# A selective scan on five engines: which products GpSimd takes, where ScalarE changes its tables, and a C of three groups

## The chip, the cores and the metric

The kernel runs on one core of a Trainium2 chip. A core has five engines with instruction queues of their own: PE (TensorE, matrix products into PSUM), DVE (VectorE), ACT (ScalarE, functions from tables), POOL (GpSimd) and SP (which issues the transfers, DMAs, here). Each works through its queue in order; semaphores tie the queues together. The metric is the device time of one execution in microseconds (us); lower is better.

## The reference, cut to what matters

The program is a chain of four layers on an image of 2 x 128 x 64 x 64. The change touches layer 0 alone, a Mamba block run over the image in four directions (the convolution and the splits written short here):

```python
def _mamba(x, W_in, conv_w, conv_b, W_xp, W_dt, b_dt, A_log, Dp, W_out):
    xz = x @ W_in.T
    xh, z = jnp.split(xz, 2, axis=-1)
    xc = causal_conv4(xh) + conv_b
    xh = silu(xc)
    dt, Bm, Cm = split(xh @ W_xp.T)          # 8, 16, 16 columns
    dt = softplus(dt @ W_dt.T + b_dt)
    A = -jnp.exp(A_log)
    dA = jnp.exp(dt[..., None] * A)
    dBu = dt[..., None] * Bm[:, :, None, :] * xh[..., None]
    h = dA_t * h + dBu_t                     # scan over L, 16 states a channel
    y = jnp.einsum('lbdn,bln->bld', hs, Cm)
    y = y + xh * Dp
    y = y * silu(z)
    return y @ W_out.T
...
x_norm = _layernorm(x_flat, ln_w, ln_b)
# four directions: rows forward, rows backward, columns forward, columns backward
fused = jnp.concatenate([out_tl_br, out_br_tl, out_tr_bl, out_bl_tr], axis=-1)
x = fused @ W_fuse.T + b_fuse
```

The length L is 4096, d_inner is 256, the batch is 2. Layers 1 and 2 are attention blocks, layer 3 a smaller Mamba.

## The kernel before

**Chunks.** Layer 0 is cut into 64 chunks of 512 positions: 2 images x 2 orders (rows, columns) x 2 senses (`rev`) x 8 chunks, one after the other in that order. The state `hst` is carried from a chunk to the next of its direction.

**Units and steps.** 256 channels x 16 states are 4096 scans; a *unit* is 1024 columns on 128 partitions (two scans of 512 side by side), so a chunk has 16 units u = 0 to 15. Unit u belongs to the group of states g = u % 8 // 2 (four states) and to the quarter of the channels q = u // 8 * 2 + u % 2. A chunk has 16 *steps*; step s contains scan s and the work that stands around it for other units. What one unit goes through:

- `s_dbu` (L381, product at L384, POOL): dbu = dus x B, for unit s + 2, into one of NDBU = 3 buffers, so that dbu(u) must wait until scan(u - 3) is done.
- `s_da` (L386, L397, ACT): da = exp(dt A), two instructions of 512, for unit s + 1, into one of two PSUM tiles, so that da(u) must wait for scan(u - 2).
- `s_fix` (L400, L412, ACT): adds the carried state at the seam into dbu(u); it needs dbu(u). For group 0 it makes `df` first (L409).
- `s_scan` (L420, L428, DVE): the scan itself, into one of NH = 3 buffers h.
- `s_hst` (L430, L433, ACT): keeps the last state, of unit s - 1.
- `s_hc` (L435): hc = h x C, of unit s - 1. For the units in `POOL_HC` POOL makes it (L438), with C as rows spread by transfers into `cs`; for the others DVE does (L440), with C in a PSUM tile `pc` that PE makes from a selection matrix (`s_pc`, L417).
- `s_y` (L447, L451, PE): adds hc into the PSUM accumulator y, two units at a time, in the step that the table `pairs` names: two steps behind a unit of DVE, three behind one of POOL. The two halves of y share one bank; `y0` (L442, L444, steps 3 and 11) begins a half with D x xs, and `yg_` (L455, L458, DVE) takes it out with the gate.

**The rest of a chunk, spread over the steps.** While chunk `c` scans, parts of the next chunk (`new`) and of the one behind it (`nxt`) are made in the same 16 steps, and the last half of `old`'s result leaves. Four tables say which: `A[s]` on ACT (behind da, fix and hst of step s), `M[s]` on PE, `V[s]` on DVE (right behind scan s) and `G[s]` on POOL. They hold: the projection of dt for `new` (`pt`, L341, PE; `abs_`, `e_exp`, `e_ln`, ACT; `dt_`, DVE; `dtu_`, POOL), the gate (`pz`, `z_`, `zsilu` in forward chunks, `zload` in backward ones), the convolution of `nxt` (`px`, L282, four products of two instructions each on PE; `x_`, L291, ACT; `xsilu`, L305, ACT; `pd`, L321, PE), the output of `old` (`po`, L469 and L473, PE; `xo`, L478 or L480, ACT), and in some chunks the layer norm (`lp`, `ln`), and `turn` (L255, 16 chunks), which lays the normed image out by columns. All PE results of this kind go through a single PSUM bank, `misc`: a product into it waits until the one before has been read. The tile `xs` of each half has two buffers for the three chunks in work, so that `nxt`'s `x_(i)` overwrites what `y0(i)` of `c` reads.

**Table visits.** ACT's exponentials all come from one table. Ln (`e_ln`, L354) and Silu (`zsilu`, L309; `xsilu`, L305) come from others; each is a visit: a load of the other table, the function, and a load back.

**Transfers.** SP spreads the rows of B and C (`states`, L331, L335: four transfers of 64 KB a group) and dt and dt x u (`spread`, L371, L376) over the partitions for `new`. C's groups are loaded in the order of `GROUPS_C`, in steps 11, 12, 13 and 15, into as many `cs` buffers.

Within a step the order of issue is: s_dbu, s_scan, V, s_hc, G, y0, s_y, s_da, s_fix, s_hst, A, M, s_pc, yg_, transfers.

Of the kernel before, what the change touches and what calls it, by code (L numbers as in the profile page):

```python
# [13 lines left out]
P = 128  # L14
B, C, H, W = 2, 128, 64, 64
L = H * W
T = 512
NCH = L // T
NS = 16
POOL_HC = (0, 5, 9, 11, 14)  # L20
GROUPS_C = (0, 2, 1, 3)
NHC, NH, NDBU = 4, 3, 3
ND3 = 6
ND = 73
# [28 lines left out]
def _bc(ap, axis, shape):  # L53
    return ap.unsqueeze(axis).to_broadcast(shape)
# [3 lines left out]
def conv_seq_kernel(ctx: ExitStack, tc: tile.TileContext, a: dict, out: bass.AP):  # L58
# [40 lines left out]
    with ExitStack() as c0:  # L99
# [9 lines left out]
        def wt(tag, bufs=None, shape=(P, 2, T)):  # L109
            return wk_.tile(list(shape), F32, tag=tag, name=tag, bufs=bufs)  # L110
# [87 lines left out]
        def gq(u):  # L198

            return u % 8 // 2, u // 8 * 2 + u % 2  # L200
# [52 lines left out]
        def turn(j):  # L253

            nc.scalar.copy(  # L255
                xnt[:, 3 + j * T : 3 + (j + 1) * T].rearrange("p (w h) -> p w h", h=H),
                xn[:, 3 : L + 3].rearrange("p (h w) -> p w h", w=W)[:, 8 * j : 8 * j + 8, :],
            )

        class Chunk:  # L260
# [69 lines left out]

            def states(self, j, g):  # L331

                t = wt("cs" if j else "bs", len(GROUPS_C) if j else 4, (P, T))
                for n in range(4):
                    nc.sync.dma_start(t[32 * n : 32 * n + 32, :],  # L335
                                      self.rows[j, 4 * g + n, :].partition_broadcast(32))
                (self.cs if j else self.bs)[g] = t
# [97 lines left out]
            def s_hc(self, u):  # L435
                t = self.hc[u] = wt("hc", NHC)
                if u in POOL_HC:
                    nc.gpsimd.tensor_mul(t, self.h[u], _bc(self.cs[gq(u)[0]], 1, [P, 2, T]))  # L438
# [51 lines left out]
        turns = {k: k % 8 for k in (*range(8, 16), *range(32, 40))}  # L490
# [3 lines left out]
        for u in range(0, 16, 2):  # L494
            pairs.setdefault(max(m + (3 if m in POOL_HC else 2) for m in (u, u + 1)), []).append(u)

        with tc.manual_schedule():
            c, c1 = chunks[:2]
# [78 lines left out]
            c.dtu_(1)  # L577
            for g in GROUPS_C:
                c.states(1, g)
# [31 lines left out]
            old = None  # L611
            for k, c in enumerate(chunks):
                new, nxt = (chunks[k + i] if k + i < nk else None for i in (1, 2))
                ln, lp = norms.get(k), norms.get(k - 1)

                def at(u):
                    return (c, u) if 0 <= u < 16 else ((old, u + 16) if u < 0 else (new, u - 16))

                A, V, M, G = {}, {}, {}, {}
                if old is not None:
                    M[2], A[4] = old.po, (old.xo,)
                if c.rev:
                    A[4] = (*A[4], c.zload)
                else:
                    A[8] = (c.zsilu,)
                if new is not None:
                    if lp is not None:
                        A[0] = (new.xd_,)  # L630
                    M[0], A[1] = lambda: new.pt(0), (lambda: new.abs_(0),)
                    M[1], A[2] = lambda: new.pt(1), (lambda: new.abs_(1), new.e_exp)
                    A[3] = (new.e_ln,)
                    M[4], V[5] = lambda: new.pt(0), lambda: new.dt_(0)
                    M[5], V[6] = lambda: new.pt(1), lambda: new.dt_(1)
                    G[7], G[8] = lambda: new.dtu_(0), lambda: new.dtu_(1)
                    if not new.rev:
                        M[6], A[7] = lambda: new.pz(0), (lambda: new.z_(0),)
                        M[13], A[14] = lambda: new.pz(1), (lambda: new.z_(1),)
                if nxt is not None:  # L640
                    M[9], A[10] = lambda: nxt.px(0), (lambda: nxt.x_(0),)
                    M[10], A[12] = lambda: nxt.px(1), (lambda: nxt.x_(1),)
                    A[13] = (nxt.xsilu,)
                    M[15] = nxt.pd
                if lp is not None:
                    A[3] = (*A[3], lp.ln, lp.exp)
                    A[6] = (lp.rows,)
                    M[7], V[8] = lp.scale, lp.mul
                    A[10] = (lp.affine, *A.get(10, ()))
                if ln is not None:  # L650
                    M[12], V[13] = ln.center, ln.sub
                    A[14] = (*A.get(14, ()), ln.square)
                    M[14], A[15] = ln.var, (ln.keep,)
                if 7 <= k < 11:
                    w1, w2 = (Low((k - 7) // 2, (k - 7) % 2, hf) for hf in range(2))
                    M[6], A[7] = w1.conv, (w1.out,)
                    M[13], A[14] = w2.conv, (w2.out, *A.get(14, ()))
                if 11 <= k < 15:
                    sl = slice(2 * T * (k - 11), 2 * T * (k - 10))
                    nc.sync.dma_start(x[:, 1, sl], xin[:, 1, sl])  # L660
                if k in turns:
                    A[11] = (lambda: turn(turns[k]),)

                for s in range(16):
                    (c1, u1), (c2, u2), (cp, up) = at(s + 1), at(s + 2), at(s - 1)

                    if c2 is not None:
                        c2.s_dbu(u2)
                    c.s_scan(s)
                    if s in V:  # L670
                        V[s]()
                    if cp is not None:
                        cp.s_hc(up)
                    if s in G:
                        G[s]()

                    if s in (3, 11):
                        c.y0(s // 11)
                    for cy, e in ((c, s), (old, s + 16)):
                        for u in pairs.get(e, ()) if cy is not None else ():  # L680
                            cy.s_y(u)
                            cy.s_y(u + 1)

                    if s == 0 and new is not None and lp is None:
                        new.xd_()
                    if c1 is not None:
                        c1.s_da(u1)
                        c1.s_fix(u1)
                    if cp is not None:
                        cp.s_hst(up)  # L690
                    for f in A.get(s, ()):
                        f()

                    if s in M:
                        M[s]()
                    if s % 2 and s < 15:
                        c.s_pc(s + 1)
                    elif s == 15 and new is not None:
                        new.s_pc(0)

                    if s == 1 and old is not None:
                        old.yg_(1)
                    if s == 10:
                        c.yg_(0)

                    if new is not None:
                        if s in (7, 14):
                            new.spread("dts", s // 14)
                        if s in (9, 13):
                            new.spread("dus", s // 13)  # L710
                        if s in (8, 10, 12, 14):
                            new.states(0, s // 2 - 4)
                        if s in (11, 12, 13, 15):
                            new.states(1, GROUPS_C[{11: 0, 12: 1, 13: 2, 15: 3}[s]])
                old = c
            c.s_hc(15)
            for e in (16, 17):
                for u in pairs.get(e, ()):
                    c.s_y(u)
                    c.s_y(u + 1)  # L720
# [12 lines left out]
    with ExitStack() as c1:  # L733
# [308 lines left out]
        for n, j in enumerate(jobs):  # L1042
# [10 lines left out]
            if jobs[n - 1].layer == 1:  # L1053
                for ci in range(NCH):
                    c = Conv(jobs[n - 1].b, ci)
# [4 lines left out]
        with tc.manual_schedule():  # L1060
# [22 lines left out]
            for slot in range((len(groups) + 2) * UPG):  # L1083
                u = slot % UPG
                G = at(slot)[0]
                if G is not None:
                    G.score(u)
                    nxt = at(slot + UPG)[0]
# [39 lines left out]
    with ExitStack() as c3:  # L1128
# [302 lines left out]
        cs = [(c, k, u) for c, k in steps for u in range(2 if k == 0 else 4)]  # L1431
# [26 lines left out]
        with tc.manual_schedule():  # L1458
            mm(y, lhsT=ident, rhs=x[:, 0, 0:T], start=True, stop=True)
            c, c1 = chunks[:2]  # L1460
# [22 lines left out]
            for s in range(-1, len(steps) + 3):  # L1483
                (pc_, pk), (cc, ck), (nc_, nk) = at(s - 1), at(s), at(s + 1)
                (n2, n2k) = at(s + 2)
                ci, k = divmod(s, 4)
                fut = chunks[ci + 1] if s >= 0 and ci + 1 < len(chunks) else None
                fut2 = chunks[ci + 2] if ci + 2 < len(chunks) else None
                old = chunks[ci - 1] if ci > 0 else None
# [216 lines left out]
```

## Time and profile before

| | us |
|---|---|
| median of 3 runs | 6571.11 (6571.02 to 6574.9) |
| the profiled execution, its own time | 6584.95 |
| its span, first to last instruction | 6583.0 |
| first scan of layer 0 to last scan of layer 0, start | 57.7 to 3468.3 |

Busy time in the stretch that holds layer 0's scans, 57 to 3470 us (3413 us):

| engine | busy us | instructions |
|---|---|---|
| PE | 2900.20 | 7790 |
| DVE | 3271.05 | 2004 |
| ACT | 2744.18 | 5241 |
| POOL | 3324.06 | 1470 |

The groups of instructions of layer 0 that matter here, on the whole span:

| line, engine, what | count | mean ns | idle before, us |
|---|---|---|---|
| L384 POOL dbu | 1024 | 2450 | 101.0 |
| L438 POOL hc | 320 | 2394 | 1.1 |
| L428 DVE scan, with a carried state | 896 | 2347 | 93.0 |
| L440 DVE hc | 704 | 1203 | 10.6 |
| L397 ACT da | 2048 | 689 | 347.6 |
| L412 ACT fix | 896 | 377 | 77.8 |
| L451 PE y | 4096 | 758 | 194.9 |

A row of the view by lines gives the source line, the engine, the number of instructions, the mean time of one, and how long the engine had been idle right before them. The view of waits names the engine that ended such idle time ("DVE h L428 <- ACT dbu L412" is a scan that waited for ACT's fix), with the total, the number and the longest. The timeline lists start, duration, engine, line and tiles, neighbours of one kind merged ("x2"), and in brackets the idle time before. Consecutive instructions of an engine overlap a little, so that the step from one start to the next is a little shorter than the duration shown.

### The profile page before, as it was taken

How to read it: one execution, taken by the hardware profiler on the slowest of the kernel's cores; microseconds unless marked ns; L12 is line 12 of the kernel's file. 1: busy time of each engine (PE TensorE's matmuls, PEld its weight loads, DVE VectorE, ACT ScalarE, POOL GpSimd, SP SyncE). 2: the span in 40 equal slices, each digit the busy share in tenths (PEclk: the TensorE clock that was granted, in tenths of full speed). 3: DMA queues.
4: the chain of work that ended last, by engine and by line, in shares of the span. 5: the costliest groups of instructions: out<-in, count | busy, mean ns of one | idle time of the engine just before them, and what ended most of it. 6: DMA issues, size and time to landing. Idle time of an engine off the chain costs nothing. (4 is left out here: it accounts for less than half of the span.)

```text
span 6583.0 us, 66639 instructions
## 1 busy us (share of the span) xinstructions
PE 5814.1 (88%) x20014; PEld 2782.5 (42%) x20014; DVE 5608.2 (85%) x4530; ACT 4490.9 (68%) x7772; POOL 5458.0 (83%) x2553
## 2 busy tenths in 40 slices
PE   8888888888888888888888999999999998788897
PEld 2222222222222222222216888888888887122221
DVE  7999999999999999999996666666666676699998
ACT  7887778877788777887776565555555555445543
POOL 6999999999999999999995666655666666688887
PEclk7888788877788777887779999999999999689888
DMA  6566655566665666556550000000000000777775
GB/s 182 146 154 161 161 142 145 147 150 150 152 152 150 151 152 151 146 145 150 149 140 19 2 4 3 1 1 1 1 1 1 1 1 1 191 176 179 186 181 135
DMA packets 400476, 700.62 MB, mean 106 GB/s; under 512 B 74089, under 2 KB 76530, under 8 KB 399730
## 3 DMA queue, kind: packets, MB, share of 16 engines
q1 hardware_dynamic: 399232, 694.33, 42.8%
q8 instruction: 157, 2.57, 0.2%
q14 instruction: 205, 1.68, 0.1%
q10 hardware_dynamic: 882, 2.04, 0.1%
HBM read 584.80 MB, written 111.28 MB: 106 GB/s over the span
## 5 line engine op out<-in xcount | busy, mean ns | idle before, releaser
L384 POOL TENSOR_TENSOR dbu<-dus,bs 128x1024 f32<-128x1024 f32 x1024 | 2464.5, 2450 | 101.0 <-DVE h L428 86.2
L428 DVE TENSOR_TENSOR_SCAN h<-da,hst,dbu 128x1024 f32<-128x1024 f32 x896 | 2096.3, 2347 | 93.0 <-ACT dbu L412 88.1
L397 ACT ACTIVATE da<-dts,aneg 128x512 f32<-128x512 f32 (+1 forms) x2048 | 1410.2, 689 | 347.6 <-DVE h L428 309.8
L924 POOL TENSOR_TENSOR sum<-sum,sc 128x1024 f32<-128x1024 f32 x384 | 910.3, 2371 | 504.1 <-ACT sc L919 500.3
L886 ACT COPY sc<-s 128x512 f32<-128x512 f32 x1024 | 596.7, 584 | 780.0 <-PE s L881 645.5
L881 PE MATMUL s<-q,k 128*128 128x256 f32 x4096 | 1052.8, 380 | 6.3 <-ACT q L838 3.0
L451 PE MATMUL y<-hc,cst 128*32 128x512 f32 x4096 | 884.9, 758 | 194.9 <-DVE hc L440 175.6
L936 PE MATMUL av<-sc,v 128*128 128x256 f32 x4096 | 1049.0, 379 | 3.6 <-ACT sc L919 3.6
L893 DVE TENSOR_TENSOR mx<-mx,s 128x512 f32<-128x512 f32 x896 | 610.2, 681 | 453.0 <-ACT sc L886 450.1
L440 DVE TENSOR_TENSOR hc<-h,pc 128x1024 f32<-128x1024 f32 x704 | 847.0, 1203 | 10.6 <-PE y L451 8.7
L881 PEld LDWEIGHTS s<-q,k 128*128 128x128 f32 x4096 | 777.3, 191 | 120.1 <-issue 6.2
L936 PEld LDWEIGHTS av<-sc,v 128*128 128x128 f32 x4096 | 768.5, 190 | 104.6 <-ACT sc L919 5.4
L438 POOL TENSOR_TENSOR hc<-h,cs 128x1024 f32<-128x1024 f32 x320 | 766.0, 2394 | 1.1 <-issue 1.1
L417 PE MATMUL pc<-xd,sel 16*128 16x512 f32 x1024 | 709.9, 784 | 1.5 <-DVE hc L440 1.3
L1323 POOL TENSOR_TENSOR A<-A,D 128x1024 f32<-128x1024 f32 x224 | 526.5, 2369 | 132.3 <-DVE D L1328 105.0
L916 DVE TENSOR_TENSOR sc<-sc,pm 128x1024 f32<-128x1024 f32 x512 | 621.1, 1214 | 0.9 <-PE pm L912 0.9
L919 ACT ACTIVATE sc<-sc 128x1024 f32<-128x1024 f32 x512 | 542.0, 1059 | 23.8 <-DVE sc L916 23.3
L341 PE MATMUL misc<-xd,w_dt 9*128 9x512 f32 x504 | 374.5, 831 | 140.3 <-ACT x L480 78.1
L451 PEld LDWEIGHTS y<-hc,cst 128*32 128x32 f32 x4096 | 125.8, 120 | 852.0 <-DVE hc L440 414.8
L412 ACT ACTIVATE dbu<-hst,dbu,df 128x1 f32<-128x1 f32 x896 | 337.9, 377 | 77.8 <-POOL dbu L384 55.5
L1340 PE MATMUL q<-xs,lc 32*128 32x512 f32 x896 | 302.0, 682 | 75.4 <-DVE A L1346 74.0
L417 PEld LDWEIGHTS pc<-xd,sel 16*128 16x128 f32 x1024 | 183.1, 219 | 351.9 <-issue 301.8
(280 smaller groups left out, 7753.8 us busy)
## 6 DMA issues: line engine op xcount, KB each, us to landing
dts<-ddt SPq DMA_DIRECT2D x512, 256.0 KB, 5.4
dus<-ddu SPq DMA_DIRECT2D x512, 256.0 KB, 5.0
D<-rows SPq DMA_DIRECT2D x448, 256.0 KB, 5.7
bs<-rows SPq DMA_DIRECT2D x1024, 64.0 KB, 4.9
cs<-rows SPq DMA_DIRECT2D x1024, 64.0 KB, 3.2
ddt<-dt SPq DMA_DIRECT2D x128, 256.0 KB, 2.0
ddu<-dtu SPq DMA_DIRECT2D x128, 256.0 KB, 4.0
dtr<-ddt SPq DMA_DIRECT2D x448, 64.0 KB, 2.1
```

The lines of the kernel that those rows point to most:

```text
L384: nc.gpsimd.tensor_mul(t, self.dus[q], _bc(self.bs[g], 1, [P, 2, T]))
L397: act(t[:, i, sl], self.dts[q][:, i, sl], AF.Exp, scale=an[:, g, 2 * q + i : 2 * q + i + 1])
L417: mm(t, lhsT=sel[32:48, 4 * g : 4 * g + 4, :].rearrange("p n d -> p (n d)"), rhs=self.xd[32:48, :], start=True, stop=True)
L428: nc.vector.tensor_tensor_scan(ho, ai, bi, init, ALU.mult, ALU.add)
L438: nc.gpsimd.tensor_mul(t, self.h[u], _bc(self.cs[gq(u)[0]], 1, [P, 2, T]))
L440: nc.vector.tensor_mul(t, self.h[u], _bc(self.pc[u // 2], 1, [P, 2, T]))
L451: mm(self.y[q // 2][r : r + 32, :], lhsT=sum4, rhs=self.hc[u][:, i, :], start=False, stop=(u % 8 >= 6), skip_group_check=True)
L881: mm(p[:, o, :], lhsT=j.k[m // 8][:, m % 8 * P : m % 8 * P + P], rhs=self.q, start=True, stop=True)
L893: nc.vector.tensor_max(self.mx, self.s[0][:, 0:2, :] if u == 1 else self.mx, self.p[u])
L916: nc.vector.tensor_sub(s, s, _bc(self.pm[:, :], 1, [P, 4, NQ]))
L924: nc.gpsimd.tensor_add(self.sum, self.s[0] if w == 1 else self.sum, self.s[w])
L936: mm(self.av, lhsT=self.job.v[m // 8][:, m % 8, :], rhs=self.s[u // 2][:, m % 4, :], start=(m == 0), stop=(m == 31))
```

## The change

- `POOL_HC` goes from units 0, 5, 9, 11, 14 to units 1, 5, 9, 13, 15. Five products stay on POOL and eleven on DVE. The pairs of y move with them: (0, 1) from step 3 to 4, (10, 11) from 14 to 13, (12, 13) from 15 to step 0 of the next chunk, (14, 15) from step 1 to step 2 of the next chunk.
- `GROUPS_C` loses group 1, whose one unit on POOL was 11. Three groups of C are spread, in steps 11, 13 and 15; the number of `cs` buffers stays four.
- `old`'s last `yg_(1)` goes from step 1 to 2, `po` from step 2 to 3; `xo` stays in step 4.
- The Ln visit (`e_ln`, and `lp.ln`, `lp.exp` where there is a norm) goes from step 3 to step 4, behind `xo`. The Silu visit of the convolution (`xsilu`) goes from step 13 to 12, and the `x_(1)` that it needs from step 12 to 11, ahead of `turn`. The visit of `zsilu` stays in step 8.

```diff
-POOL_HC = (0, 5, 9, 11, 14)
-GROUPS_C = (0, 2, 1, 3)
+POOL_HC = (1, 5, 9, 13, 15)
+GROUPS_C = (0, 2, 3)
...
-                t = wt("cs" if j else "bs", len(GROUPS_C) if j else 4, (P, T))
+                t = wt("cs" if j else "bs", 4, (P, T))
...
-                    M[2], A[4] = old.po, (old.xo,)
+                    M[3], A[4] = old.po, (old.xo,)
                 if c.rev:
-                    A[4] = (*A[4], c.zload)
+                    A[4] = (*A.get(4, ()), c.zload)
...
-                    A[3] = (new.e_ln,)
+                    A[4] = (*A.get(4, ()), new.e_ln)
...
                     M[9], A[10] = lambda: nxt.px(0), (lambda: nxt.x_(0),)
-                    M[10], A[12] = lambda: nxt.px(1), (lambda: nxt.x_(1),)
-                    A[13] = (nxt.xsilu,)
+                    M[10], A[11] = lambda: nxt.px(1), (lambda: nxt.x_(1),)
+                    A[12] = (nxt.xsilu,)
                     M[15] = nxt.pd
                 if lp is not None:
-                    A[3] = (*A[3], lp.ln, lp.exp)
+                    A[4] = (*A[4], lp.ln, lp.exp)
...
-                    A[11] = (lambda: turn(turns[k]),)
+                    A[11] = (*A.get(11, ()), lambda: turn(turns[k]))
...
-                    if s == 1 and old is not None:
+                    if s == 2 and old is not None:
                         old.yg_(1)
...
-                        if s in (11, 12, 13, 15):
-                            new.states(1, GROUPS_C[{11: 0, 12: 1, 13: 2, 15: 3}[s]])
+                        if s in (11, 13, 15):
+                            new.states(1, GROUPS_C[(s - 11) // 2])
...
-            for e in (16, 17):
+            for e in (16, 17, 18):
                 for u in pairs.get(e, ()):
                     c.s_y(u)
                     c.s_y(u + 1)
```

## The prediction

> **What bounds the kernel now.** I read the table by window first, then the waits of each engine inside layer 0, then one stretch of the timeline. A steady 500 us of layer 0, as busy time of PE, PEld, DVE, ACT and POOL, granted clock and DMA share:
>
> ```profile
> 1500.00:2000.00 500.00, 424.97 (x1132) 114.83 (x1134) 478.91 (x292) 405.84 (x768) 489.73 (x217) 0.79 0.62 150
> ```
>
> GpSimd (489.7) and VectorE (478.9) are both nearly full, so neither can gain much: the first scan starts at 57.7 us, the last chunk's at 3420.6, so a chunk takes (3420.6 - 57.7)/63 = 53.38 us, and GpSimd is busy 489.73/500 of it, 52.3 us. Its number of instructions does not change, so 52.3 us is the floor and about 1.1 us a chunk the most there is to win. The lost time stands in the waits (total, times, longest):
>
> ```profile
> DVE h L428 <- ACT dbu L412: 88.1, 124, 1.7
> POOL dbu L384 <- DVE h L428: 85.8, 98, 1.3
> ACT xs L291 <- PE misc L282: 104.9, 55, 3.8
> ACT xs L291 <- PE y L444: 64.7, 55, 2.0
> ```
>
> VectorE's scans wait for ScalarE's fix of the carry (L412), and GpSimd waits for a scan to give a dbu buffer back. The last two lines are the ones to keep in mind: ScalarE waits for PE at both halves of the convolution, x_(0) and x_(1). Sorted by their place in the chunk (averages over 58 chunks), the scan waits lie at scan 5 (0.52 us a chunk) and scan 15 (0.75): each is the first scan behind a table visit. The visit behind step 3, in one chunk:
>
> ```profile
> 1518.72 0.39 ACT L412 ACTIVATE dbu<-hst,dbu,df 128x1 f32<-128x1 f32 x1 [0.43 <-POOL dbu L384]
> 1519.01 0.18 ACT L433 COPY hst<-h 128x2 f32<-128x2 f32 x1
> 1519.19 1.28 ACT L354 ACT_TABLE_LOAD   x1
> ...
> 1522.86 1.42 ACT L397 ACTIVATE da<-dts,aneg 128x511 f32<-128x511 f32 x2
> ...
> 1524.61 2.35 DVE L428 TENSOR_TENSOR_SCAN h<-da,hst,dbu 128x1024 f32<-128x1024 f32 x1 [0.36 <-ACT dbu L412]
> ```
>
> GpSimd's product dbu(4) is late, so fix(4) is, then the visit (3.67 us from 1519.19 to 1522.86), da(5) and fix(5) (1.75 us to the scan), and scan 5; its end frees the buffer for dbu(8). This loop sets the period. Steps between starts in this chunk, used below: scan 2.26 (1524.61 to 1526.88), dt_ or yg_ 0.58, hc on VectorE 1.11 (1516.31 to 1517.42), dbu 2.38 (two in 4.77), hc on GpSimd 2.31 (1529.41 to 1531.72), dtu 1.23 (1534.07 to 1535.30). The loop: from dbu(8) to the next chunk's dbu(4) GpSimd makes 13 dbu, 5 hc, 2 dtu = 30.94 + 11.55 + 2.46 = 44.95; fix to table load 0.47; visit 3.67; da and fix 1.75; scan 2.26: 53.10 against the measured 53.38. So this reading accounts for the time.
>
> **The change, part by part.**
>
> *The log visit, step 3 to 4.* It now stands behind fix(5) and shares step 4 with xo. GpSimd's chain to dbu(5) is followed by fix 0.47, xo 0.83 (1524.57 to 1525.40), the visit 3.67 and da(6), fix(6) 1.75 = 6.72 us, and step 5 has dt_ on VectorE too, which covers 0.58. Taken alone with the new products, the longest loop I find runs from scan 13's end: 6 dbu and 3 hc (21.21), 6.72, and VectorE from scan 6 to the end of scan 13 (24.74) = 52.67, that is 0.43 less than the 53.10. So this part alone would win about 0.4 us a chunk. The wait of scan 5 (0.52) and of dt_(0) for PE (0.09) go.
>
> *x_(1) from step 12 to 11, xsilu from 13 to 12.* This is the part that decides. One chunk's stretch around it:
>
> ```profile
> 1538.17 2.35 DVE L428 TENSOR_TENSOR_SCAN h<-da,hst,dbu 128x1024 f32<-128x1024 f32 x1
> ...
> 1540.16 5.52 PE L282 MATMUL misc<-xnt,wk 128*128 128x512 f32 x8
> ...
> 1545.72 0.69 ACT L291 ACTIVATE xs<-misc,vec 128x512 f32<-128x512 f32 x1 [3.37 <-PE misc L282]
> ...
> 1546.67 3.70 PE L282 MATMUL misc<-xnt,wk 128*128 128x512 f32 x8
> ...
> 1547.93 0.18 ACT L433 COPY hst<-h 128x2 f32<-128x2 f32 x1
> 1548.02 1.41 ACT L397 ACTIVATE da<-dts,aneg 128x511 f32<-128x511 f32 x2
> ...
> 1550.21 1.02 PE L444 MATMUL y<-xs,diag_d 128*128 128x512 f32 x2
> ...
> 1551.27 0.69 ACT L291 ACTIVATE xs<-misc,vec 128x512 f32<-128x512 f32 x1 [1.45 <-PE y L444]
> 1551.85 1.41 ACT L397 ACTIVATE da<-dts,aneg 128x511 f32<-128x511 f32 x2
> ...
> 1553.65 1.28 ACT L305 ACT_TABLE_LOAD   x1
> ...
> 1557.41 1.42 ACT L397 ACTIVATE da<-dts,aneg 128x511 f32<-128x511 f32 x2
> ...
> 1559.17 4.59 DVE L428 TENSOR_TENSOR_SCAN h<-da,hst,dbu 128x1024 f32<-128x1024 f32 x2 [1.27 <-ACT dbu L412]
> ```
>
> Scan 9 starts at 1538.17. PE makes px(0) behind the y products of hc(7); x_(0) reads the one "misc" bank, px(1) needs that bank back, and x_(1) also overwrites the xs buffer that y0(1) (L444) reads. So x_(1) cannot start before px(1) and y0(1) are through: 4.9 us after x_(0)'s end, on average over the chunks, and never under 4.6. ScalarE needs only 1.8 us of that for da(12), fix and hst; already a step later it waits 1.45 here. In step 11 it stands right behind the hst of 1547.93, with da(13) queued behind it, and waits about 3.1 us, until 1551.27. Scan 13 waits for that da(13), and scan 14 for the visit that follows. From 1551.85 on ScalarE does what it does now with every unit one lower: da(13) where da(14) is, xsilu at 1553.65 as now, da(14) at 1557.41. So scan 14 starts at 1559.17, where scan 15 starts today. The table visit has been put earlier in order, not in time.
>
> *What a chunk is then worth.* Before, scan 15 starts at 1559.17, the next chunk's scan 0 2.26 later (hc(14) is GpSimd's), its scan 6 on average 21.2 later: 23.46. After: scans 14 and 15 and hc(14) on VectorE 2.26 + 2.26 + 1.11 = 5.63; to scan 6: six scans 13.56, four hc 4.44 (hc 15, 1 are GpSimd's; 0, 2, 3, 4 remain), yg_ and dt_ 1.16 = 19.16; in all 24.79. GpSimd's path from scan 14's end is longer: 2.26, then dbu 1 to 5 and hc 15, 1 (11.9 + 4.62 = 16.52), then the 6.72 above = 25.50. Scan 6 to scan 9 is as before. So a chunk grows by 25.50 - 23.46 = 2.04. The bounds of this part: the stall is covered and the 0.43 above is all, or GpSimd, ScalarE and PE are each late in turn and a chunk pays 3.6 (scan 0's own shift of 5.63 - 2.26 = 3.37, and a little of po). I take 2.04, which follows rows of this stretch all the way.
>
> *po behind y0(0), in step 3.* yg_(1) ends 14.1 us behind scan 14's start (scan 2 starts at 11.25). y0(0) and the six po matmuls took 5.3 to 5.7 us on PE in the trace when they began from a pause; xo, wanted at 19.3, would then wait 0.1 to 0.5, or nothing if PE is quicker. I take 0.15. Sum: 2.2 us a chunk.
>
> The Trainium skill, page "TensorE: Matmul & The Clock Gate" (Part 1: The HAM clock gate), says that PE runs at half rate until about 3.4 us of sustained work have passed. The rows of px(0), 5.52 us, and px(1), 3.70 us, for the same eight instructions agree. By the rule a warm px(0) would bring x_(1) 1.8 us forward and the sum would be 0.4 a chunk; by the row it is 2.2.
>
> *turn.* In 16 chunks a 1.1 us copy (L255) now stands behind x_(1) in step 11, ahead of da(13), where before it filled ScalarE's wait: 16 x 1.1 = 18 us; bounds 0 and 18.
>
> *C of three groups.* Four of 32 row transfers a chunk go (256 issues of 64 KB). GpSimd's hc waited 0.0 us for them, so they win nothing; the fourth buffer stays and SP waits less. The most they could give is the 0.6 us in all that GpSimd waits for DMA. The number of products on each engine is the same, 5 and 11: no change of work.
>
> *Sum.* 62 chunks have an x_ of a later one: 62 x 2.2 = 136, plus 18 = 154 us on the profiled 6583.0, so 6737; its run of 6584.95 lies 13.8 above the median of 6571.11, so 6571 + 154 = 6725. ScalarE's visits keep their number and price: first load to next work 3.67 us.
>
> The Trainium skill, page "ScalarE: Activation LUTs" (What ACT_TABLE_LOAD costs), gives 2.66 us for each switch, with a drain of 1.38 behind the load. The rows show 1.28 and the next instruction at once. By the page a visit would cost 6.4 and scan 6 would be some 2.7 us later a chunk; the sum goes by the row.
>
> **The rivals.**
>
> *Faster.* If PE is through px(1) in time, only the log visit's gain is left: 63 x -0.43 = -27, so 6544. For it: scan 5's wait is real and the loop over dbu(4) is the period. Against it: x_(1) already waits 1.2 us on average one step later. It decides if the time from x_(0)'s end to x_(1) falls under about 2.5 us.
>
> *Slower still.* yg_(1) late for s_y(14, 15) of GpSimd's hc(15), po behind y0(0), the log visit behind both, so that fix(6) slips another 1.4 us: 62 x 3.6 + 18 = 241, so 6812. For it: PE at a clock of 0.79 and "PE misc L469 <- ACT" waits today. Against: 2 us of slack ahead of yg_(1). It decides from xo waiting over 1 us.
>
> *Even.* x_(1) comes 2.2 us sooner than in the stretch above, and the log visit's gain pays for what is left of the stall: 6571. For it: PE's rows vary (eight instructions in 5.52 us and in 3.70). Against: the shortest time from x_(0) to x_(1) over all chunks is 4.65 us, the mean 4.9, so the spread is on px(0)'s side, and px(0) at px(1)'s pace brings 1.8.
>
> **How the numbers follow.** Forecast 0.73; slower still 0.12; even 0.05; faster 0.10. The likeliest is 6725. The range begins where px(0) runs at px(1)'s 3.70 us (2.2 - 1.8 = 0.4 a chunk, and turn: 6571 + 43 = 6614) and ends at 6800, just under the slower rival: it leaves out the even and faster cases and the upper part of that rival. Within 0.2% (13 us) a measurement of this kernel can hardly tell a difference; slower 0.85, same 0.05, faster 0.10.
>
> **What would show it.** Scans waiting for ScalarE's fix in steps 13 and 14 instead of 5 and 15, some 3 us a chunk (total near 200 us against 88); L291's wait for "PE y L444" up from 65 to about 190 us; VectorE and GpSimd both busy some 4% less of a window; GpSimd waiting for scans 3 us a chunk, at dbu(1) and near it; a chunk of 55.6 us. Wrong would be a wait at L291 that stays near 65 us, or a chunk under 53.4 us in spite of it: then something else hid the stall.

## The result, and the profile after

The changed kernel takes 6897.42 us (median of 4 runs, 6895.77 to 6899.3) against 6573.0 for the one before in the same comparison: ratio 1.0496, 95% interval 1.0484 to 1.0509. It is slower by 324 us, where the prediction had 154, and lies above its range. Two time units are used below: a chunk is one of the 64 passes of 16 steps, and "us a chunk" is a mean over 58 of them, sorted by place from the trace. A chunk took 53.4 us before and takes 58.4 now; the layers behind layer 0 take the same time (3112 us before, 3114 after).

A steady 500 us of layer 0, in the view by windows (PE, PEld, DVE, ACT and POOL busy, granted clock, DMA share, GB/s):

```profile
1500.00:2000.00 500.00, 394.62 (x1040) 105.52 (x1038) 443.56 (x270) 353.89 (x666) 448.10 (x200) 0.74 0.54 133
```

All five engines are less busy than in the same window before (POOL 448 against 490 us, DVE 444 against 479). No engine has become the bound: they wait for each other. The view of waits in layer 0, engine by engine, from 115 to 3640 us (total, times, longest):

```profile
DVE h L428 <- ACT dbu L412: 270.6, 193, 3.0
DVE dt L458 <- PE y L451: 84.6, 61, 3.2
POOL dbu L384 <- DVE h L428: 330.0, 305, 4.1
ACT xs L291 <- PE y L444: 191.2, 60, 3.4
ACT x L480 <- PE misc L473: 69.5, 45, 2.9
ACT x L478 <- PE misc L473: 27.4, 16, 2.6
```

The fourth line is the stall of x_(1) as it was forecast (65 us before, 191 now). The second and the last two are not in the forecast's sum, but for 0.15 us a chunk at xo: yg_(1) waits for the y products of units 14 and 15 (12.8 us before), and xo waits for po (almost never before). By place, the scans wait 1.6 us a chunk at scan 13, 2.0 at scan 14 and 1.1 at scan 6, yg_(1) 1.3, hc(0) 0.3 and scan 1 0.3; at scans 5 and 15 nothing is left.

The stretch around x_(1), of one chunk in the timeline:

```profile
1641.68 0.69 ACT L291 ACTIVATE xs<-misc,vec 128x512 f32<-128x512 f32 x1 [3.52 <-PE misc L282]
...
1642.62 3.70 PE L282 MATMUL misc<-xnt,wk 128*128 128x512 f32 x8
...
1643.89 0.18 ACT L433 COPY hst<-h 128x2 f32<-128x2 f32 x1
...
1646.16 1.02 PE L444 MATMUL y<-xs,diag_d 128*128 128x512 f32 x2
...
1647.22 0.69 ACT L291 ACTIVATE xs<-misc,vec 128x512 f32<-128x512 f32 x1 [3.15 <-PE y L444]
1647.80 1.41 ACT L397 ACTIVATE da<-dts,aneg 128x511 f32<-128x511 f32 x2
...
1649.56 2.35 DVE L428 TENSOR_TENSOR_SCAN h<-da,hst,dbu 128x1024 f32<-128x1024 f32 x1 [2.01 <-ACT dbu L412]
1649.61 1.28 ACT L305 ACT_TABLE_LOAD   x1
...
1655.12 4.59 DVE L428 TENSOR_TENSOR_SCAN h<-da,hst,dbu 128x1024 f32<-128x1024 f32 x2 [2.11 <-ACT dbu L412]
```

ScalarE is through with the hst at 1644.07 and stands until 1647.22 (3.15 us), with da(13) behind it. Scan 13 waits 2.01 us for that da, and scan 14 another 2.11 us for the Silu visit that follows. The head of the next chunk, in the same view:

```profile
1662.20 2.38 POOL L438 TENSOR_TENSOR hc<-h,cs 128x1024 f32<-128x1024 f32 x1
...
1664.83 0.58 ACT L348 ACTIVATE e<-misc 128x512 f32<-128x512 f32 x1
...
1665.47 1.22 PE L341 MATMUL misc<-xd,w_dt 9*128 9x512 f32 x1 [3.06 <-ACT e L348]
...
1667.47 1.94 PE L451 MATMUL y<-hc,cst 128*32 128x512 f32 x8
...
1669.48 0.69 DVE L458 TENSOR_TENSOR dt<-sz,y 128x512 f32<-128x512 f32 x1 [0.78 <-PE y L451]
...
1670.22 2.08 PE L444 MATMUL y<-xs,diag_d 128*128 128x512 f32 x2 [0.81 <-DVE dt L458]
...
1672.09 1.92 PE L469 MATMUL misc<-x,cst 128*128 128x512 f32 x2
...
1673.81 2.02 PE L473 MATMUL misc<-dt,wof 128*128 128x512 f32 x4
...
1675.87 1.06 ACT L480 COPY x<-misc 128x512 f32<-128x512 f32 x1 [1.41 <-PE misc L473]
...
1676.95 1.28 ACT L354 ACT_TABLE_LOAD   x1
...
1682.37 2.35 DVE L428 TENSOR_TENSOR_SCAN h<-da,hst,dbu 128x1024 f32<-128x1024 f32 x1 [1.22 <-ACT dbu L412]
```

GpSimd is through with hc(15) at 1664.58, but the y products that need it start at 1667.47: on PE they stand behind pt(1), which had waited 3.06 us for ScalarE's abs_(0) to read the bank "misc". yg_(1) is 0.78 late; y0(0) waits for yg_(1), po stands behind y0(0), xo waits 1.41 for po, the log visit stands behind xo, and scan 6 is 1.22 late.

### The profile page after: what moved, and what is told of

It reads as the page before. It is cut to its first block, busy times and chain, and to the rows that moved or that the text cites. A ratio compares the mean times of both kernels' runs of the same rounds, so it can differ in the third digit from the quotient of the medians.

```text
span 6893.7 us, 66330 instructions
## 1 busy us (share of the span) xinstructions
PE 5878.3 (85%) x20014; PEld 2803.1 (41%) x20014; DVE 5618.8 (82%) x4530; ACT 4509.3 (65%) x7772; POOL 5449.0 (79%) x2553
## 3 DMA queue, kind: packets, MB, share of 16 engines
q10 hardware_dynamic: 882, 2.04, 0.1%
## 5 line engine op out<-in xcount | busy, mean ns | idle before, releaser
L384 POOL TENSOR_TENSOR dbu<-dus,bs 128x1024 f32<-128x1024 f32 x1024 | 2441.9, 2404 | 422.1 <-DVE h L428 335.0
L428 DVE TENSOR_TENSOR_SCAN h<-da,hst,dbu 128x1024 f32<-128x1024 f32 x896 | 2090.6, 2342 | 280.6 <-ACT dbu L412 277.1
L451 PE MATMUL y<-hc,cst 128*32 128x512 f32 x4096 | 858.9, 791 | 166.4 <-DVE hc L440 119.4
```

Source lines behind the costliest of these rows:

```text
L384: nc.gpsimd.tensor_mul(t, self.dus[q], _bc(self.bs[g], 1, [P, 2, T]))
L428: nc.vector.tensor_tensor_scan(ho, ai, bi, init, ALU.mult, ALU.add)
L451: mm(self.y[q // 2][r : r + 32, :], lhsT=sum4, rhs=self.hc[u][:, i, :], start=False, stop=(u % 8 >= 6), skip_group_check=True)
```

## The experiments

The three parts of the change, as I took them apart: the *convolution part* (x_(1) to step 11, the Silu visit to 12), the *log part* (the visit to step 4) and the *products part* (POOL_HC, pairs, C of three groups, yg_(1) to step 2, po to step 3). Theories: *stall* (the convolution part pays nearly all), *products* (the later y, yg_ and po pay), *log* (the visit behind xo pays); in the later runs *ring* stands for the chain of turns on the "misc" bank and PE's queue. Each result is given as a ratio to the kernel before on the same chip in the same comparison; "= n us" is that ratio less 1, times 6573.

**conv_back**: the changed kernel without the convolution part.

```diff
-                    M[10], A[11] = lambda: nxt.px(1), (lambda: nxt.x_(1),)
-                    A[12] = (nxt.xsilu,)
+                    M[10], A[12] = lambda: nxt.px(1), (lambda: nxt.x_(1),)
+                    A[13] = (nxt.xsilu,)
```

> The changed kernel with x_(1) back in step 12 and the Silu visit back in step 13; products, C groups, yg_, po and the log visit stay changed. Stall theory (ScalarE stands at x_(1) for PE and everything behind is one unit late): x_(1)'s wait falls from 191 to about 65 us, scans 13 and 14 wait under 0.5 us a chunk, chunk 52.7 to 53.4 us, time 6535 to 6575. Products theory (hc(15) on GpSimd, with yg_(1) and po a step later, makes VectorE and ScalarE wait for PE): the waits of yg_(1) (85 us) and xo (97 us) stay, chunk 55 to 56, time 6680 to 6740. Log theory (the visit behind xo pays): scan 6 keeps its 1 us, time near 6640.

Measured: 6721.97, ratio 1.0191 (1.0171 to 1.0212) = 126 us. So the convolution part costs 326 - 126 = 200 us on top of the others, and the rest costs 126, where the stall theory had a gain. The time is that of the products theory; the sign of the log theory, scan 6 waiting 1.1 us a chunk, stays as well. L291's wait is back at 66 us, and xo's is the largest new one of ScalarE:

```profile
ACT x L480 <- PE misc L473: 96.0, 47, 12.0
ACT xs L291 <- PE y L444: 66.3, 55, 2.0
```

**conv_only**: the kernel before with the convolution part alone (the same edit the other way, with `turn` behind x_(1)).

> The kernel before with x_(1) in step 11 and the Silu visit in step 12, nothing else. Stall theory: x_(1) waits about 3.1 us a chunk, scan 13 then waits 2.9 and scan 14 2.2 us, scan 0 of the next chunk comes 3.4 us later, of which scan 5's wait gives back 0.3: 62 x 3.1 + 18 = 210, time about 6780. Products theory and log theory: within 30 us of before, 6570 to 6600.

Measured: 6871.54, ratio 1.0413 (1.0390 to 1.0437) = 271 us. Scans 13 and 14 wait 2.4 and 2.0 us a chunk; 2.9 and 2.2 were expected. That the time is 61 us above the 210 expected lies in a wait that was not foreseen: xd_ (L326) waits for PE's pd, because hc(13), and with it the y products of units 12 and 13 ahead of pd on PE, come later (pd begins 0.2 us ahead of scan 0, in the kernel before 1.8), and scan 1 waits 1.9 us a chunk behind it.

```profile
ACT xd L326 <- PE misc L321: 216.4, 59, 5.1
```

**x1_only**: x_(1) to step 11 alone; the Silu visit stays in step 13.

```diff
-                    M[10], A[12] = lambda: nxt.px(1), (lambda: nxt.x_(1),)
+                    M[10], A[11] = lambda: nxt.px(1), (lambda: nxt.x_(1),)
...
-                    A[11] = (lambda: turn(turns[k]),)
+                    A[11] = (*A.get(11, ()), lambda: turn(turns[k]))
```

> The kernel before with x_(1) in step 11 and nothing else; the Silu visit stays in step 13, the products and y stay. Stall theory: ScalarE stands at x_(1) for 3.1 us with da(13) behind it, scan 13 waits 2.4 to 2.9 us a chunk, scan 14 none, scan 15 about 1.2: 2.2 a chunk, 62 x 2.2 + 18 = 154, time about 6730 where before is 6575 to 6590. If only the Silu visit's place costs (conv_only had both): scan 13's wait is given back at scan 15, within 40 us of before.

Measured: 6734.52, ratio 1.0246 (1.0224 to 1.0268) = 162 us, with 154 expected. Scan 13 waits 2.5 us a chunk, scan 14 nothing, scan 15 only 0.3; in place of the 0.9 missing there, 1.4 us lie at step 1, again behind xd_, so that the sum agrees partly by luck:

```profile
ACT xs L291 <- PE y L444: 191.1, 61, 3.4
ACT xd L326 <- PE misc L321: 124.0, 55, 3.8
```

One instruction of 0.69 us, moved one step forward in its queue (and in 16 chunks turn, which now stands behind it), costs 2.5%.

**silu_12_only**: the changed kernel with x_(1) back in step 12, right ahead of the Silu visit, which stays.

```diff
-                    M[10], A[11] = lambda: nxt.px(1), (lambda: nxt.x_(1),)
-                    A[12] = (nxt.xsilu,)
+                    M[10], A[12] = lambda: nxt.px(1), (lambda: nxt.x_(1), nxt.xsilu)
```

> The changed kernel with x_(1) back in step 12, right ahead of the Silu visit, which stays there. Stall theory: da(13) no longer stands behind x_(1), scan 13 waits under 0.3 us a chunk instead of 1.6; scan 14 waits about 1.7; a chunk 1.6 to 1.9 shorter, time 6780 to 6800. If the visit's place alone is what costs: within 30 us of 6897.

Measured: 6736.5, ratio 1.0227 (1.0212 to 1.0243) = 149 us, that is 177 less than the changed kernel; 97 to 117 less was expected. Scan 13 waits nothing, scan 14 1.6 us. What is more than expected is yg_(1), which waits 0.8 in place of 1.3: when the tail of a chunk is earlier, the wait at the head of the next shrinks too. conv_back, with the visit back as well, is only 23 us better: with x_(1) in step 12, the Silu visit's place is worth little. That holds only there: on the kernel before, conv_only (x_(1) and the visit moved) costs 271 - 162 = 109 us more than x1_only. So x_(1)'s move costs by itself, and it makes the visit's move costly too; how much belongs to each depends on which is counted first.

**log_only**: the kernel before with the log visit in step 4.

```diff
-                    A[3] = (new.e_ln,)
+                    A[4] = (*A.get(4, ()), new.e_ln)
...
-                    A[3] = (*A[3], lp.ln, lp.exp)
+                    A[4] = (*A[4], lp.ln, lp.exp)
```

> The kernel before with the log visit in step 4 behind xo, nothing else. Stall theory: scan 5's wait (0.52 us a chunk) goes, scan 6 waits under 0.2, chunk 52.6 to 53.1, time 6525 to 6560. Log theory: fix(6) comes late, scan 6 waits 1 us a chunk, time 6600 to 6640.

Measured: 6547.98, ratio 0.9931 (0.9914 to 0.9949) = -45 us: faster than both kernels. A chunk takes 52.8 us; scan 5's wait is gone, scan 6 waits 0.09. GpSimd is busy 494.5 of 500 us:

```profile
1500.00:2000.00 500.00, 417.04 (x1140) 113.88 (x1138) 485.89 (x298) 410.76 (x777) 494.51 (x220) 0.79 0.61 148
```

**products_only**: the kernel before with the products part alone (the changed kernel with the convolution and the log part taken back).

> The kernel before with the new products, three groups of C, yg_(1) in step 2 and po in step 3; all three table visits and x_(1) as before. Stall theory: GpSimd is no longer late at dbu(4), chunk 52.7 to 53.2, time 6530 to 6570. Products theory: yg_(1) waits 1.3 us a chunk for PE and xo 1.5, time 6650 to 6740.

Measured: 6673.84, ratio 1.0122 (1.0104 to 1.0141) = 80 us: the products theory's time. yg_(1) waits as in the changed kernel, while xo, with the log visit ahead of it in step 3, hardly waits (20 us):

```profile
DVE h L428 <- ACT dbu L412: 88.4, 85, 2.0
DVE dt L458 <- PE y L451: 83.1, 59, 3.4
```

Alone, the log part brings 45 us. On top of the products part it costs 126 - 80 = 46 (conv_back against products_only). With po a step later, xo is late, and the visit behind xo with it: scan 6 waits 1.1 us a chunk in conv_back and not at all here.

**y_before_pt**: the changed kernel with the y products of units 14 and 15 in step 1, ahead of pt(1) on PE.

```diff
-            pairs.setdefault(max(m + (3 if m in POOL_HC else 2) for m in (u, u + 1)), []).append(u)
+            pairs.setdefault(max(m + (3 if m in POOL_HC and m < 15 else 2) for m in (u, u + 1)), []).append(u)
```

> The changed kernel with the y products of units 14 and 15 one step earlier on PE (ahead of pt(1), which waits for ScalarE's abs_(0) to free the one bank); GpSimd still makes hc(15). Ring theory (they are late because they stand behind pt(1)): yg_(1)'s wait falls from 85 us to under 25, xo's wait for po from 97 to about 50, a chunk gets 1.3 to 1.9 us shorter, time 6780 to 6820. Slow-PE theory (PE is late there whatever the order, at a clock of 0.83): the wait of yg_(1) stays above 60 us, time 6870 to 6900.

Measured: 6828.2, ratio 1.0370 (1.0353 to 1.0388) = 243 us, 83 less than the changed kernel; just above the ring theory's span as a time, within it by the ratio (6816 where before is 6573). yg_(1)'s wait falls from 84.6 to 4.6 us and xo's from 97 to 60, a chunk from 58.4 to 57.2:

```profile
DVE dt L458 <- PE y L451: 4.6, 11, 0.4
ACT x L480 <- PE misc L473: 39.9, 41, 1.9
ACT x L478 <- PE misc L473: 20.3, 15, 2.7
```

So for yg_(1) the order on PE decides. Part comes back elsewhere: pt(1) now waits behind y, and scan 4 waits 0.4 us a chunk.

**y0_behind_po**: the changed kernel with y0(0) issued behind po.

```diff
-                    if s in (3, 11):
-                        c.y0(s // 11)
+                    if s == 11:
+                        c.y0(1)
...
                     if s in M:
                         M[s]()
+                    if s == 3:
+                        c.y0(0)
```

> The changed kernel with y0(0) issued behind po in step 3 instead of ahead of it. If po's place behind y0(0) is what makes xo, the log visit and fix(6) late: xo's wait falls from 97 us to about 40, scan 6's from 1.0 to 0.4 us a chunk, time 6840 to 6865. If po is late because yg_(1) is: xo's wait falls by less than 20 us, time within 15 us of 6897.

Measured: 6777.51, ratio 1.0302 (1.0281 to 1.0322) = 199 us, 127 less than the changed kernel, more than twice the expected 32 to 57. yg_(1) still waits (74 us), but xo no longer, and scan 6's wait of 1.1 us a chunk is gone:

```profile
DVE h L428 <- ACT dbu L412: 198.1, 136, 3.0
DVE dt L458 <- PE y L451: 74.2, 56, 3.2
```

xo had waited 97 us over 61 chunks, 1.6 each; a chunk got 1.9 shorter. VectorE's idle time fell at scan 6 (1.1), dt_ (0.2), yg_(1) (0.2) and scan 13 (0.25).

**all_but_conv**: convolution part taken back, and both PE orders mended.

> x_(1) and the Silu visit back in steps 12 and 13, and both PE orders mended (y of 14, 15 ahead of pt(1), y0(0) behind po); products, C groups and log visit as changed. Ring theory: the waits of yg_(1) and xo are gone, what stays is scan 15's 0.8, chunk 52.7 to 53.3, time 6530 to 6570, beside 6548 for the log visit alone. If the products themselves cost (GpSimd's three hc between steps 14 and 2): time 6600 to 6660.

Measured: 6645.85, ratio 1.0085 (1.0067 to 1.0103) = 56 us, the second of the two answers. yg_(1)'s wait is gone and xo's down to 34 us, 12 of them behind the last chunk, but the products part still leaves it 101 us above log_only. VectorE idles 2.9 us a chunk (1.7 in log_only): scan 15 1.1, step 1 0.65, scan 6 0.4, dt_ 0.35. That GpSimd's hc(13) and hc(15) take work from VectorE just where ScalarE is late would fit this; it was not tried by itself and stays open.

**log_pool10**, **log_pool1_10**: an attempt to make log_only better.

```diff
-POOL_HC = (0, 5, 9, 11, 14)
+POOL_HC = (0, 5, 9, 10, 14)      # log_pool10
+POOL_HC = (1, 5, 9, 10, 14)      # log_pool1_10
```

> The kernel before with the log visit in step 4, and GpSimd's product of unit 11 given for that of unit 10 (0, 5, 9, 10, 14), so that no product of units 11 to 13, which stand behind the Silu visit, is off VectorE. Window theory (a visit costs nothing when the three hc behind it are VectorE's): scan 15's wait falls from 0.79 us a chunk to under 0.4, chunk 52.3 to 52.7, 15 to 30 us under log_only, time 6515 to 6535 on a chip where before is 6571. If GpSimd, busy 52 of 53 us, is the bound, or dbu(14) now comes too late: within 10 us of log_only or above it.

> As log_pool10, with unit 1 in place of unit 0 on GpSimd. Window theory: the same gain, within 10 us of log_pool10. If moving a product within steps 0 to 2 costs by itself (scan 1 and hc(0) waited 0.65 us in all_but_conv): 20 to 40 us slower than log_pool10.

Measured: 1.0087 (1.0072 to 1.0101) = 57 us and 1.0062 (1.0048 to 1.0075) = 41 us, against log_only's -45: a miss. The window theory looked at table visits alone. ScalarE is late at x_(0) too, in step 10, and hc(10) was VectorE's work there; without it scan 12 waits 0.7 us a chunk, and the Silu visit is no earlier, because fix(14) now waits for dbu(14): of the 55 us in the last line 45 lie there. In log_only the fixes wait 71 us in all, but none of it there. Later still xd_ waits 107 us for PE (27 in log_only) and holds scan 1:

```profile
ACT xd L326 <- PE misc L321: 107.5, 54, 4.1
DVE h L428 <- ACT hst L433: 75.6, 64, 2.9
ACT dbu L412 <- POOL dbu L384: 55.0, 53, 2.6
```

The second case of log_pool1_10, a cost of 20 to 40 us, is not met: unit 1 in place of 0 costs nothing by itself.

**four_groups**: the changed kernel with all four groups of C spread (group 1 is read by nobody).

```diff
-GROUPS_C = (0, 2, 3)
+GROUPS_C = (0, 2, 1, 3)
...
-                        if s in (11, 13, 15):
-                            new.states(1, GROUPS_C[(s - 11) // 2])
+                        if s in (11, 12, 13, 15):
+                            new.states(1, GROUPS_C[{11: 0, 12: 1, 13: 2, 15: 3}[s]])
```

> The changed kernel with all four groups of C spread by transfers again (the one of group 1 is read by nobody). If the transfers are covered: within 15 us of 6897 (ratio to before 1.047 to 1.052). If the transfers that were dropped had cost time: 30 us or more slower.

Measured: 6894.85, ratio 1.0478 (1.0464 to 1.0492), against 1.0496 (1.0484 to 1.0509): the transfers that were dropped cost nothing that can be seen.

## Why the prediction was wrong

- **The bound of the kernel before: right.** The loop over dbu(4), the log visit and scan 5 was said to set the period. log_only breaks it: scan 5's wait goes, a chunk gets 0.55 us shorter, the time 45 us, and GpSimd then stands at 494.5 of 500 us busy. The gain of 0.43 a chunk, 27 us, was worked out for the visit's move together with the new products, though, and so it is not borne out: with these, in conv_back, there is a loss of 126 us.
- **x_(1): right in mechanism and place, near in size.** The stall was put at 3.1 us (measured 3.15 in the chunk shown), scan 14 at the time of scan 15. From the start of scan 9, scan 15 came 20.05 us later before and scan 14 comes 20.46 later now; from there to scan 0 5.63 were worked out and 5.61 measured. The scans wait 3.6 us a chunk at steps 13 and 14, 3 were said. Alone, x_(1) costs 162 us; within the change the convolution part costs 200, where 2.04 + 0.43 a chunk and turn make 171.
- **The step that failed: "po behind y0(0), in step 3", taken at 0.15 us a chunk, with "2 us of slack ahead of yg_(1)".** From scan 0 to scan 6, 25.65 - 5.63 = 20.02 us were worked out; 22.64 were measured. These 2.6 us in 62 chunks are 162 us, and the whole miss is 326 - 154 = 172. (Of what is left, 0.4 us a chunk is scan 14's being later than scan 15 was; 0.2 go the other way, as the base of 23.46 took 2.26 from scan 15 to scan 0, where the kernel before needs 2.44 on average.) The PE work itself was sized well: y0(0) and po take 5.6 us in the chunk shown, 5.3 to 5.7 were said. What was wrong is when they can begin. No working is given for the slack; it comes out at about 2 us if the y products begin at hc(15)'s end, 9.33 behind scan 14's start by the steps of the prediction (9.46 in the chunk shown). That leaves out that the y products of 14 and 15 had gone behind pt(1) in PE's queue, and that pt(1) waits for abs_(0): in the chunk shown they begin 2.9 us behind hc(15)'s end. abs_(0) itself begins only half a us later than before, 5.3 us behind scan 0 against 4.9. y_before_pt takes yg_(1)'s wait away (83 us), y0_behind_po xo's (127 us); from scan 0 to scan 6 they are 0.75 and 1.5 us a chunk shorter than the changed kernel. The two together were run only without the convolution part: there (all_but_conv) 56 us are left of conv_back's 126, where the forecast's terms for these parts, the 0.15 left out, give -27. So late PE work is the larger part of the miss and not all of it; what the rest of the products part costs stays open.
- **Its consequence.** The log part was credited with 0.43 inside the change. There it costs: with xo late, the visit behind xo is late too (-45 us alone, +46 on top of the products).
- **The slower rival** named this mechanism, yg_(1) late and po behind y0(0), at 6812 with a chance of 0.12. It should have been the forecast, and even so was priced too low (6897 measured).
- **C of three groups at nothing, turn at up to 18 us:** four_groups bears out the first. The second was not measured by itself.
- **The stall theory of the expectations, that the products part is a gain, fell** with products_only (+80 us).
- **The pace of PE behind a pause.** y0(0)'s two products took 2.08 us behind a wait of 0.81, and the same form takes 1.02 in the tail of the chunk, where PE had been running; the mean granted clock of the execution fell from 0.865 to 0.831. The rule of the Trainium skill that the prediction named ("TensorE: Matmul & The Clock Gate", Part 1: The HAM clock gate), half rate until some 3.4 us of sustained work have passed, fits these two rows; no run here separates its share of the miss from the waits themselves.

## What to carry to other kernels

Moving an instruction forward in an in-order queue brings its work forward only if its inputs are ready there; if not, it carries its wait to everything behind it. Before such a move, read the idle time in front of the instruction in its old place: x_(1) already waited 1.2 us there, and a step earlier it waits 3.1. And when a product moves a step later, write down what now stands ahead of each of its followers on every queue, and which of those wait for an engine that the same change makes late: here one bank of PSUM tied PE and ScalarE into a chain of turns, and the log visit's move, which wins 45 us by itself, costs 46 on top of the products part, where po has moved too.

## What the runs showed of the hardware that was not expected

GpSimd's product dbu took 2404 ns on average in the changed kernel and 2450 before, with the same instruction, which looks as if GpSimd ran faster when VectorE idles more. Most of it is a matter of counting: an instruction that follows another without idle time overlaps with it, dbu by 86 ns on average before and 65 now, and such dbu are fewer now (549 against 829 in 58 chunks). With overlaps counted once, GpSimd is busy for 52.0 us a chunk before, 51.8 in the changed kernel, 52.0 in log_only and 52.1 in conv_only, though VectorE idles between 1.7 and 7.0 us a chunk in them. So GpSimd's busy time a chunk is a floor that held at all these loads, and the 52.3 of the prediction, from one window, is close to it. The scan on VectorE takes 2347 ns before, 2342 now and 2340 in log_only, where GpSimd is busiest: it does not follow GpSimd's load.
